# Row statistics of two layer norms, from bn_stats on VectorE to sums on VectorE and squared deviations on ScalarE

## The chip, the cores and the metric

The kernel runs on one core of a Trainium2 chip. The metric is the device time of one execution in microseconds, lower is better. A core has TensorE (PE, with its weight loads shown apart as PEld), VectorE (DVE), ScalarE (ACT), GpSimd (POOL) and SyncE (SP, which here only issues DMAs). Each engine works through its own instructions in order; engines wait for each other through semaphores.

## The reference

Sixteen graphs (batches) of 1024 nodes with 256 features pass through two graph layers, each followed by a residual and a layer norm over the 256 features:

```python
e_k   = leaky(einsum('bid,bjd->bij', h * a_k, h))            # layer 0
alpha = sigmoid(where(adj == 1, e_0, -max)); ...             # adj is 0 or 1 here
x = layernorm(x + einsum('bij,bjd->bid', alpha, h) + bias)
Hh = x @ W                                                   # layer 1
e  = where(adj != 0, exp(-leaky_relu(s[:, None] + d[None, :])), 0)
x = layernorm(x + elu(e @ Hh / rowsum(e)))
def layernorm(x): m = mean(x); v = var(x); return (x - m) / sqrt(v + 1e-5)
```

A row has one mean and one variance in each of the two norms. There are 16 x 1024 rows, that is 16 x 8 tiles of 128 rows, for each norm.

## The kernel before

The order of the work is written out by hand: every engine's instructions stand in the order in which the Python code calls them. The main loop is over batches b = 1 to 15. One turn of the loop does layer 0 of batch b beside layer 1 of batch b - 1 (`prev`) and the end of batch b - 2 (`done`):

1. **Strips** (L757 to L796, jt = 0 to 7). PE computes one strip of scores (L254), upper triangle only; ACT takes two tanh of it (L262 `tb`, L263 `low`); DVE takes the maximum (L264), applies the mask (L270, `finish`) and turns 32 x 32 blocks (L290, `dump`). SP writes the turned strip to DRAM (`mir<-tb`) and one strip later reads it back as the mirrored lower triangle (`al<-mir`, L298, `gather`). Beside it PE projects tiles of `prev` (L558) and ACT evicts them (`project`, `evict_H`: L568 to L570 and L579).
2. **Products** (L816 to L853). Layer 0's sum is a 2 x 2 block product with seven multiplications (L453, banks pQ, pV, pR, pW). DVE masks the gathered blocks (L305, `mask`), combines blocks (L431) and adds up the results (`unite`: L473, L484, L486). The bank pW is used twice: DVE must have read it (L486, `unite(b, "s")`) before PE's product 4 writes it again. Beside it ACT scales tiles of earlier batches (L364) and counts adjacency entries (L130, `check_adj`, a Square with an accumulated sum), and DVE forms layer 1's weights (L619).
3. **Sums** (L856 to L906, t = 0 to 7). PE sums layer 1 of `prev` in eight tiles (L624); the first three are computed together. For each tile DVE inverts the row sum (L660, L661), ACT takes relu and exp (`elu`: L669, L670), and DVE makes the row y = elu + x1 in two instructions (`add`: L675, L677) and then its statistics (`stats`: bn_stats L326, bn_aggr L328). After t = 3 and t = 5 DVE makes the statistics of four tiles of layer 0's rows of batch b (`stats0`, again L326 and L328) and POOL turns them into 1 / sqrt(variance + eps) and the factors that `project` needs (`roots0`: L335 to L359, L401).

`load_adj(b + 1, 1, ...)` at t = 5 issues a load of half of the next adjacency matrix on POOL's queue; a one-element copy (L104) from POOL's own `r_all` makes it wait its turn.

In the last turn (b = 15) there is no next batch: `stats0` and `roots0` come at t = 2 and 3, the projection of batch 15 itself at t = 4 and 6 (its banks come from the pools of the `acc` tiles: tile t = 7 of `acc` gets the bank that the projection's tile 4 had, after ACT's L579 has evicted that), and L600 sends a row of factors through DRAM before the last weights. Then layer 1 of batch 15 runs alone, and `done` = 14 is finished beside it.

Batch 0 is done ahead of the loop (`end0`) and keeps bn_stats in both versions, as do the second norm's rows of batch 15.

Of the kernel before, what the change touches and what calls it, by code (L numbers as in the profile page):

```python
# [10 lines left out]
BF16 = mybir.dt.bfloat16  # L11
U16 = mybir.dt.uint16
I32 = mybir.dt.int32
AF = mybir.ActivationFunctionType
ALU = mybir.AluOpType
AX = mybir.AxisListType
PSUM = bass.MemoryType.PSUM

P = 128
# [4 lines left out]
EPS = 1e-5  # L24
LOW = 1.0e-14
CHECKS = 4
# [4 lines left out]
def one_kind_pass(  # L31
# [296 lines left out]
            nc.vector.bn_aggr(mv, st)  # L328
        return st

    def rstd(mv, what, add_eps=EPS):

        n_t = mv.shape[1]
        ve = small.tile([P, NT], F32, tag="ve", name=f"ve_{what}")[:, 0:n_t]
        nc.gpsimd.tensor_scalar(ve, mv[:, :, 1], add_eps, None, ALU.add)  # L335
        return root_of(ve, what)

    def root_of(ve, what):

# [10 lines left out]

    r_all = {}

    def center(mv, what, add_eps=EPS):

        r = rstd(mv, what, add_eps)
        n = mv.shape[1]
        mr = small.tile([P, NT], F32, tag="mr", name=f"mr_{what}")[:, 0:n]
        nc.gpsimd.tensor_tensor(mr, mv[:, :, 0], r, ALU.mult)
        nc.gpsimd.tensor_scalar(mr, mr, -1.0, None, ALU.mult)  # L359
        r_all[what] = r  # L360
        return [(r[:, t : t + 1], mr[:, t : t + 1]) for t in range(n)]

# [32 lines left out]
    def stats0(b, t):  # L395
        stats(x1s[b][:, t, :], mv0s[b][:, t, :], f"0_{b}_{t}")

    def roots0(b, g):
        r0s[b] += center(mv0s[b][:, ts(g, HT), :], f"0_{b}_{g}", 4.0 * EPS)
        for k, f in enumerate((1.0, -SLOPE, SLOPE - 1.0)):  # L400
            nc.gpsimd.tensor_scalar(  # L401
                rcols[b][:, k, ts(g, HT)], r_all[f"0_{b}_{g}"], f, None, ALU.mult
            )
# [268 lines left out]
    def add(b, t, between=None):  # L672

        y = ys[b][t]
        nc.vector.scalar_tensor_tensor(y, y, 1.0, hs[b, t], ALU.min, ALU.add)  # L675
        if (b, t) != (B - 1, NT - 2):
            nc.vector.scalar_tensor_tensor(y, y, -1.0, x1s[b][:, t, :], ALU.add, ALU.add)  # L677
        if between:
            between()

        full = (b, t) == (B - 1, NT - 2)
        return stats(y, None if full else mv1s[b][:, t, :], f"1_{b}_{t}")

    def scale1(b, t):
        scale(ys[b][t], *r1s[b][t])
# [63 lines left out]
    for b in range(1, B):  # L749
        prev, done = b - 1, b - 2  # L750
        last = b == B - 1

        projects = [[0, 1], [2], [3], [4, 5], [6, 7], [], [], []]
        if prev == 0:

            projects = [[], [], [0, 1], [2, 3], [4, 5, 6, 7], [], [], []]
        for jt in range(NT):  # L757
            if jt == 4:
                mask(b, 0, 0, HT)
                combine_al(b, 1, 0, 2)  # L760
            if jt == 5:
                new_yT(b)
                product(b, 1)
                share_p(prev)
                mask(b, 1, 0, HT)
                combine_al(b, 1, 2, 3)
                mask(b, 0, HT)
                mask(b, 1, HT)
                mask(b, 2, 0, HT)
                combine_al(b, 1, 3, HT)  # L770
                mask(b, 2, HT)
                if done >= 0:
                    r1s[done] = center(mv1s[done], f"1_{done}")
            if jt == 6:
                unite(b, "p1")
                product(b, 5)
                unite(b, "p5")
                mask(b, 3, HT)
                combine_al(b, 2, 0, HT)
            strip(b, jt)  # L780
            finish(b, jt, ends=False)
            if jt < NT - 1:
                dump(b, jt)
            if prev == 0 and jt == 0:
                turn_x1(0, 0)
            if prev == 0 and jt == 1:
                transpose_x1(0)
            if jt >= 1:
                gather(b, jt - 1)
            if jt < 4:  # L790
                combine_x(b, jt)
            for t in projects[jt]:
                project(prev, t)
            if jt == 4:
                evict_H()
            add_twice(b, jt)  # L796
        if not last:
            new_xT(b + 1)
            load_blocks(xTs[b + 1], x[b + 1], 0, N)

        def extras(n):
            if prev == 0 and n < 2:
                scale0(0, HT + 2 * n)
                scale0(0, HT + 2 * n + 1)
            elif prev > 0:
                scale0(prev, 2 * n)
                scale0(prev, 2 * n + 1)
            if done >= 0:
                for q in (2 * n, 2 * n + 1):
                    scale1(done, q)  # L810
                    if q in (3, 7):
                        store(done, q - 3, HT)
            if n < 3:
                check_adj(b, n)

        product(b, 3)  # L816
        combine_al(b, 3, 0, HT)
        extras(0)
        product(b, 6)
        weights(prev, 0)  # L820
        mask(b, 4)
        mask(b, 5)
        combine_al(b, 4, 0, 2)
        weights(prev, 1)
        mask(b, 6)
        combine_al(b, 4, 2, HT)
        unite(b, "u2")
        extras(1)
        product(b, 7)
        extras(2)  # L830
        product(b, 2)
        extras(3)
        unite(b, "s")
        unite(b, "c12")
        unite(b, "c22")
        unite(b, "c11")
        product(b, 4)
        turn_y(b, 0)
        weights(prev, 2)
        weights(prev, 3)  # L840
        weights(prev, 4)
        unite(b, "c21")
        turn_y(b, 1)
        fetch_y(b, 0)
        fetch_y(b, 1)
        if not last:
            load_x(b + 1, [nc.sync])
        check_adj(b, 3)
        weights(prev, 5)
        weights(prev, 6)  # L850
        weights(prev, 7)
        check_pq(prev)
        if not last:  # L853
            load_adj(b + 1, 0, behind=x1s[b][:, HT, 0:1])

        def sum_of(t):  # L856
            homes = {"a": (ps_acc, "acc"), "e": (ps_e, "e"), "t": (ps_t, "t")}
            return acc1(prev, t, *homes[("aaeteeaa" if last else "aaeettat")[t]])

        n_first = 3  # L860
        first = [sum_of(t) for t in range(n_first)]
        for m in range(NT):
            for t in range(n_first):
                sum1(prev, t, first[t], m)
        if not last:
            turn_x(b + 1, 0, False)
            turn_x(b + 1, 1, False)
        rinvs = invert_sums(prev, first)
        for t in range(NT):
            if t >= n_first:  # L870
                acc = sum_of(t)
                for m in range(NT):
                    sum1(prev, t, acc, m)
            if last and t == 7:
                for m in range(4):
                    weights(b, m, 0, HT)
            elu(prev, t, *((first[t], rinvs[t]) if t < n_first else (acc,)))
            if last and t in (2, 3):
                for q in range(HT):
                    stats0(b, (t - 2) * HT + q)  # L880
                roots0(b, t - 2)
            if t >= 1:
                add(prev, t - 1)
            if not last and t in (3, 5):
                for q in range(HT):
                    stats0(b, (t - 3) // 2 * HT + q)
                roots0(b, (t - 3) // 2)
                if t == 5:
                    load_adj(b + 1, 1, behind=r_all[f"0_{b}_1"][:, 0:1])
            if t == 3 and not last:  # L890
                scale_x(b + 1, 0)
                scale_x(b + 1, 1)
            if last and t in (4, 6):
                t0 = (t - 4) // 2 * HT
                for n in range(HT):
                    project(b, t0 + n)
                evict_H()
                share_half(b, t0)
            if last and t in (5, 7):
                for q in range(HT):  # L900
                    scale0(b, (t - 5) // 2 * HT + q)
            if last and t == 7:
                for m in range(4, 6):
                    weights(b, m, 0, HT)
        if not last:
            add(prev, NT - 1)  # L906
# [25 lines left out]
    for m in range(NT):  # L932
        if m in (3, 4):
            weights(last, m + 3, 0, HT)
        if m == 4:
            add(done, NT - 1)
            r1s[done] = center(mv1s[done], f"1_{done}")

        for k in range(3 * m - 15, min(3 * m - 12, NT)) if m >= 5 else []:
            weights(last, k, HT, HT)  # L940
        for t in range(n_first):
            sum1(last, t, first[t], m)
# [484 lines left out]
```

## Time and profile before

| what | value |
|---|---|
| runs | 1222.68, 1223.67, 1224.05 us (median 1223.67) |
| the profiled execution: its time | 1222.76 us |
| its span, first to last instruction | 1221.0 us (clock granted 0.998 of full speed) |
| busy: DVE / ACT / POOL | 1080.9 / 729.9 / 362.8 us |
| bn_stats, L326: y_kept, x (120 and 128 of them) | 428 and 397 ns each |
| bn_aggr, L328 (254) | 182 ns each |
| `add`'s second instruction, L677 (120, y_kept) | 425 ns each |
| `check_adj`, L130, 128 x 2048 (64) | 1991 ns, and a read of the accumulator of 190 ns |
| DMA queues: share of 16 engines' span | 56.1% (SP's issues) and 18.5% (POOL's) |

The span is what the instructions fill; 1.76 us of the execution lie around it. Busy shares are means over the whole run. In a timeline the columns are: start, length (both in us, of a merged row for all its xN instructions), engine, line, operation, out<-in, and in brackets the idle time of the engine before it with what ended it. ACT instructions overlap a little: the next can start before the last ends.

### The profile page before, as it was taken

How to read it: one execution, taken by the hardware profiler on the slowest of the kernel's cores; microseconds unless marked ns; L12 is line 12 of the kernel's file. 1: busy time of each engine (PE TensorE's matmuls, PEld its weight loads, DVE VectorE, ACT ScalarE, POOL GpSimd, SP SyncE). 2: the span in 40 equal slices, each digit the busy share in tenths (PEclk: the TensorE clock that was granted, in tenths of full speed). 3: DMA queues.
4: the chain of work that ended last, by engine and by line, in shares of the span. 5: the costliest groups of instructions: out<-in, count | busy, mean ns of one | idle time of the engine just before them, and what ended most of it. 6: DMA issues, size and time to landing. Idle time of an engine off the chain costs nothing.

```text
span 1221.0 us, 15690 instructions
## 1 busy us (share of the span) xinstructions
PE 1209.4 (99%) x4400; PEld 820.0 (67%) x4400; DVE 1080.9 (89%) x2075; ACT 729.9 (60%) x1686; POOL 362.8 (30%) x730
## 2 busy tenths in 40 slices
PE   9999999999999999999999999999999999999997
PEld 7757657576575766758667485675757657576686
DVE  5699898998989989898998989989899898998867
ACT  4573664656657466574666736666475665746654
POOL 2320333412334122332213333133241233412343
PEclk9999999999999999999999999999999999999999
DMA  9567776798778877787887868878688887787412
GB/s 194 104 132 149 136 151 147 154 180 147 142 159 152 183 140 148 151 158 165 160 165 138 157 142 163 171 135 160 141 165 176 147 148 155 152 186 137 106 52 73
DMA packets 604600, 180.66 MB, mean 148 GB/s; under 512 B 482012, under 2 KB 586968, under 8 KB 604504
## 3 DMA queue, kind: packets, MB, share of 16 engines
q1 hardware_dynamic: 582800, 136.90, 56.1%
q0 software_dynamic: 21008, 42.01, 18.5%
q8 instruction: 37, 0.61, 0.2%
q10 hardware_dynamic: 696, 0.66, 0.2%
q14 instruction: 59, 0.48, 0.1%
HBM read 152.44 MB, written 60.62 MB: 175 GB/s over the span
## 4 chain that ended last, share of the span: by engine, by line
PE 92%; DVE 5%; ACT 1%; DMA 1%; issue 1%; SPq 0%; POOL 0%; ACTq 0%; DVEq 0%; POOLq 0%
PE acc L624 33%; PE pe L254 20%; PE pW L453 9%; PE pV L453 8%; PE pH L558 8%; PE pQ L453 7%; PE pR L453 4%; PE acc L381 2%; DVE e L619 1%; DVE al L431 1%; DVE st L326 1%; DMA al<-mir 0%; DVE yT L486 0%; DVE yT L473 0%; DMA p<-p_row 0%
## 5 line engine op out<-in xcount | busy, mean ns | idle before, releaser
L624 PE MATMUL acc<-H,e 128*128 128x257 f32 x2032 | 444.5, 380 | 0.0
L624 PEld LDWEIGHTS acc<-H,e 128*128 128x128 f32 x2032 | 385.3, 190 | 62.5 <-issue 7.2
L254 PE MATMUL pe<-xa,xT 128*128 128x384 f32 (+1 forms) x720 | 249.5, 486 | 0.0
L254 PEld LDWEIGHTS pe<-xa,xT 128*128 128x128 f32 x720 | 132.8, 190 | 89.7 <-issue 54.3
L284 POOL TENSOR_TENSOR al<-ident,al 128x128 f32<-128x128 f32 x128 | 105.9, 836 | 285.9 <-DVE al L270 285.8
L619 DVE SCALAR_TENSOR_TENSOR e<-p,pq_kept,adj 128x1024 f32<-128x1024 f32 (+1 forms) x136 | 161.1, 1229 | 0.5 <-DMA p<-p_row 0.5
L431 DVE TENSOR_TENSOR al<-al 128x1024 f32<-128x1024 f32 (+2 forms) x105 | 145.5, 1386 | 8.3
L262 ACT ACTIVATE tb<-pe 128x512 f32<-128x512 f32 (+1 forms) x192 | 94.2, 491 | 86.7 <-PE pe L254 80.4
L669 ACT ACTIVATE h<-acc,rinv 128x256 f32<-128x256 f32 x81 | 38.3, 473 | 155.8 <-DVE rinv L661 155.8
L264 DVE TENSOR_TENSOR tb<-tb,low 128x512 f32<-128x512 f32 (+1 forms) x192 | 103.0, 550 | 27.7 <-ACT low L263 27.5
L130 ACT ACTIVATE junk<-adj,minus 128x2048 bf16<-128x2048 bf16 x64 | 127.4, 1991 | 0.0
L558 PE MATMUL pH<-Wx,yT 128*128 128x258 f32 x480 | 116.3, 380 | 0.0
L104 POOL CAST adj<-x 128x1 bf16<-128x1 f32 x15 | 2.8, 188 | 369.2 <-DMA x<-y_rows 262.8
L558 PEld LDWEIGHTS pH<-Wx,yT 128*128 128x128 f32 x480 | 91.2, 190 | 31.1 <-issue 13.4
L453 PE MATMUL pV<-al,S 128*128 128x512 f32 x240 | 108.4, 594 | 1.2 <-ACT tb L262 0.5
L453 PE MATMUL pW<-al,x 128*128 128x512 f32 x240 | 108.8, 596 | 0.4
L453 PE MATMUL pQ<-al,x 128*128 128x512 f32 x240 | 107.9, 592 | 0.0
L270 DVE SCALAR_TENSOR_TENSOR al<-tb,adj 128x512 f32<-128x512 f32 (+7 forms) x132 | 97.8, 741 | 5.0
L263 ACT ACTIVATE low<-pe 128x512 f32<-128x512 f32 (+1 forms) x192 | 93.6, 487 | 1.2 <-DVE tb L264 1.2
L650 ACT ACTIVATE sums<-acc,tiny 128x1 f32<-128x1 f32 x45 | 11.8, 261 | 126.3 <-PE acc L624 126.3
L305 DVE SCALAR_TENSOR_TENSOR al<-al,adj 128x512 f32<-128x512 f32 (+3 forms) x150 | 80.9, 560 | 6.2 <-DMA al<-mir 5.7
L453 PEld LDWEIGHTS pW<-al,x 128*128 128x128 f32 x240 | 44.7, 190 | 60.7 <-issue 49.7
(146 smaller groups left out, 1572.3 us busy)
## 6 DMA issues: line engine op xcount, KB each, us to landing
adj<-in_adjT POOLq DMA_DIRECT2D x30, 1024.0 KB, 8.5
x<-in_x SPq DMA_DIRECT2D x15, 1024.0 KB
y_rows<-Z SPq DMA_DIRECT2D x240, 64.0 KB, 2.0
x<-y_rows SPq DMA_DIRECT2D x30, 512.0 KB, 4.8
out<-y_kept SPq DMA_DIRECT2D x30, 512.0 KB, 3.4
xT<-in_x SPq DMA_DIRECT2D x112, 128.0 KB, 3.9
p<-p_row POOLq DMA_DIRECT2D x15, 512.0 KB, 4.1
mir<-tb SPq DMA_DIRECT2D x60, 112.0 KB, 3.3
```

Of the source, the lines that this page charges most:

```text
L130: nc.scalar.activation(junk, rows, AF.Square, bias=minus1, scale=2.0, accum_out=chk[:, b * CHECKS + n : b * CHECKS + n + 1],)
L254: nc.tensor.matmul(pe[:, 0:w], lhsT=xTs[b][:, c, ts(jt, P)], rhs=xas[b][:, c, ds(jt * P + o, w)], start=(c == 0), stop=(c == ND - 1),)
L262: nc.scalar.activation(tb[:, ds(o, w)], pe[:, 0:w], AF.Tanh, scale=0.5)
L263: nc.scalar.activation(low[:, 0:w], pe[:, 0:w], AF.Tanh, scale=0.5 * SLOPE)
L264: nc.vector.tensor_tensor(tb[:, ds(o, w)], tb[:, ds(o, w)], low[:, 0:w], ALU.max)
L270: nc.vector.scalar_tensor_tensor(als[b][:, jt, c0:c1], tbs[b, jt][:, c0 - jt * P : c1 - jt * P], 1.0, adjs[b, jt // HT][:, jt % HT, c0:c1] ...
L284: nc.gpsimd.tensor_tensor(diag, ident2, diag, ALU.add)
L431: nc.vector.tensor_tensor(out_, in0, in1, ALU.subtract)
L453: nc.tensor.matmul(banks[bank], lhsT=lhs[:, jt, :], rhs=rhs[:, jt, :], start=first and jt == 0, stop=jt == HT - 1, skip_group_check=True,)
L558: nc.tensor.matmul(pt, lhsT=x1Ts[b][:, c, ts(t, P)], rhs=Wx[:, c, :], start=(c == 0), stop=(c == ND - 1),)
L619: nc.vector.scalar_tensor_tensor(e, p_bcs[b][:, cols], q, rows, ALU.mult, ALU.min)
L624: nc.tensor.matmul(acc, lhsT=es[b][:, m, ts(t, P)], rhs=Hs[b][m], start=(m == 0), stop=(m == NT - 1),)
```

## The change

Statistics of the eight tiles of the first norm (batches 1 to 15) and of the second norm (batches 0 to 14) change their form; 240 tiles in all. For the first norm, DVE makes the row sums of four tiles with one reduction (`sums0`). For the second, the second instruction of `add` also gives the row sum as an accumulated output. For both, ACT then computes the sum of squares of (sum - 256 times the row) with one Square with an accumulated sum (`deviation`). The division by 256 is left to `rstd` and `center` on POOL (`unit`). A tile's deviation stands, in ACT's order, later than its sum: at t for the second norm's tile t - 2 (the last two tiles after strips 0 and 1 of the next turn), and two of the first norm's tiles at each of t = 4 to 7. `roots0` moves from t = 3 and 5 to t = 5 and 7. In the last turn four deviations stand at each of t = 2 and 3. The copy ahead of `load_adj(b + 1, 1)` reads a sum of the second half instead of a root, so it no longer stands behind `roots0` on POOL's queue.

All deviations write their unneeded squares to one scratch tile with the tag `tmp`, which `check_adj` uses too. The built order shows that a deviation therefore waits for ACT's own semaphore, that is for the deviation just before it.

The order of PE's and SP's instructions is the same in both versions. DVE has 480 instructions fewer of bn_stats and bn_aggr and 30 reductions more; ACT has 240 deviations more.

```diff
-    def rstd(mv, what, add_eps=EPS):
+    def rstd(mv, what, add_eps=EPS, unit=1.0):
...
-        nc.gpsimd.tensor_scalar(ve, mv[:, :, 1], add_eps, None, ALU.add)
+        if unit == 1.0:
+            nc.gpsimd.tensor_scalar(ve, mv[:, :, 1], add_eps, None, ALU.add)
+        else:
+            nc.gpsimd.tensor_scalar(ve, mv[:, :, 1], unit * unit * unit, add_eps, ALU.mult, ALU.add)
         return root_of(ve, what)
+
+    def deviation(y, sums):
+
+        junk = one.tile([P, NT // CHECKS, N], BF16, tag="tmp", name="dev_junk")
+        nc.scalar.activation(
+            junk[:, 0, 0:D],
+            y,
+            AF.Square,
+            bias=sums[:, 0:1],
+            scale=-1.0 * D,
+            accum_out=sums[:, 1:2],
+        )
...
-    def center(mv, what, add_eps=EPS):
-
-        r = rstd(mv, what, add_eps)
+    def center(mv, what, add_eps=EPS, unit=1.0):
+
+        r = rstd(mv, what, add_eps, unit)
...
-        nc.gpsimd.tensor_scalar(mr, mr, -1.0, None, ALU.mult)
+        nc.gpsimd.tensor_scalar(mr, mr, -unit, None, ALU.mult)
...
+    def sums0(b, g):
+        nc.vector.tensor_reduce(
+            mv0s[b][:, ts(g, HT), 0], x1s[b][:, ts(g, HT), :], AX.X, ALU.add
+        )
+
+    def deviation0(b, t):
+        deviation(x1s[b][:, t, :], mv0s[b][:, t, :])
+
     def roots0(b, g):
-        r0s[b] += center(mv0s[b][:, ts(g, HT), :], f"0_{b}_{g}", 4.0 * EPS)
+        unit = 1.0 / D if b else 1.0
+        r0s[b] += center(mv0s[b][:, ts(g, HT), :], f"0_{b}_{g}", 4.0 * EPS, unit)
...
         nc.vector.scalar_tensor_tensor(y, y, 1.0, hs[b, t], ALU.min, ALU.add)
+        if b < B - 1:
+            nc.vector.scalar_tensor_tensor(
+                y, y, -1.0, x1s[b][:, t, :], ALU.add, ALU.add, accum_out=mv1s[b][:, t, 0:1]
+            )
+            return None
...
+    def deviation1(b, t):
+        deviation(ys[b][t], mv1s[b][:, t, :])
...
-                    r1s[done] = center(mv1s[done], f"1_{done}")
+                    r1s[done] = center(mv1s[done], f"1_{done}", unit=1.0 / D)
...
             if jt < NT - 1:
                 dump(b, jt)
+            if jt < 2 and done >= 0:
+                deviation1(done, NT - 2 + jt)
...
             elu(prev, t, *((first[t], rinvs[t]) if t < n_first else (acc,)))
             if last and t in (2, 3):
+                sums0(b, t - 2)
                 for q in range(HT):
-                    stats0(b, (t - 2) * HT + q)
+                    deviation0(b, (t - 2) * HT + q)
                 roots0(b, t - 2)
             if t >= 1:
                 add(prev, t - 1)
+            if t >= 2:
+                deviation1(prev, t - 2)
             if not last and t in (3, 5):
-                for q in range(HT):
-                    stats0(b, (t - 3) // 2 * HT + q)
-                roots0(b, (t - 3) // 2)
+                sums0(b, (t - 3) // 2)
                 if t == 5:
-                    load_adj(b + 1, 1, behind=r_all[f"0_{b}_1"][:, 0:1])
+                    load_adj(b + 1, 1, behind=mv0s[b][:, HT, 0:1])
+            if not last and t >= 4:
+                for q in range(2 * t - 8, 2 * t - 6):
+                    deviation0(b, q)
+                if t % 2 == 1:
+                    roots0(b, (t - 5) // 2)
...
         if m == 4:
             add(done, NT - 1)
-            r1s[done] = center(mv1s[done], f"1_{done}")
+            for q in (NT - 2, NT - 1):
+                deviation1(done, q)
+            r1s[done] = center(mv1s[done], f"1_{done}", unit=1.0 / D)
```

## The prediction

> **What bounds the kernel now.** I read the page first, then the chain of waits in order of time, then the timelines of ACT, DVE and PE over one turn of the loop. The page:
>
> ```profile
> PE 1209.4 (99%) x4400; PEld 820.0 (67%) x4400; DVE 1080.9 (89%) x2075; ACT 729.9 (60%) x1686; POOL 362.8 (30%) x730
> PE 92%; DVE 5%; ACT 1%; DMA 1%; issue 1%; SPq 0%; POOL 0%; ACTq 0%; DVEq 0%; POOLq 0%
> ```
>
> PE is busy nearly always. Whether it works at its pace is read from repetitions. In the chain of waits:
>
> ```profile
> 551.08 27.81 PE acc L624 x128
> ...
> 625.50 27.81 PE acc L624 x128
> ...
> 700.72 27.81 PE acc L624 x128
> ```
>
> The sums take 27.81 us in each turn, so nothing stalls inside them. From one such line to the next is a turn: 74.42 us here, 75.22 us in the next. The 14 distances (the first line at 102.88, the last at 1149.35 us) are 74.42 to 74.48 six times, else 75.45, 75.00, 75.22, 75.11, 74.78, 74.45, 74.59, 75.28. Above 74.42 that is **4.6 us in all: no more can be won inside the loop**, however much DVE is relieved. [...]
>
> Where those 4.6 us go: to DVE, late before product 4. From the timelines of PE and DVE:
>
> ```profile
> 621.91 3.60 PE L453 MATMUL pW<-al,x 128*128 128x512 f32 x8
> ```
>
> ```profile
> 620.83 0.74 DVE L486 SCALAR_TENSOR_TENSOR yT<-pW,bcol,yT 128x512 f32<-128x512 f32 x1
> 682.15 0.69 DVE L305 SCALAR_TENSOR_TENSOR al<-al,adj 128x512 f32<-128x512 f32 x1 [0.88 <-DMA al<-mir]
> ```
>
> PE may write pW when L486 has read it. It starts at best 70.99 us after the sums' first matmul (550.92); where it starts later, it does so 0.06 us after L486's end. So the deadline for that end is 70.93. L486 ends, in the 14 turns, at 71.85, 71.41, 70.64, 70.72, 70.61, 70.89, 70.65, 71.62, 71.52, 71.19, 70.72, 70.85, 71.00, 71.69. Seven miss it, mostly through a late gather (the second line, 0.88 us in the turn from 625.34); the others have 0.04 to 0.32 us left.
>
> **The relief of DVE.** Per turn go 8 x (428 + 182) and 8 x (397 + 182) ns, 9.5 us; two reductions of 128 x 1024 come, at 1.23 us (L431 reads as many elements), no dearer than four times 420 ns (L189, 256 elements): 2.5 us. The accumulated output of L677 is not in this trace: between nothing and one small instruction (182 ns, L328); I take 0.1 us, 0.8 us a turn. Net some 6 us a turn, all in the sums. (The reduction waits for the same fetched rows as bn_stats, which at 567.54 waited for nothing; it comes about 1 us sooner, and a wait there would come out of the relief.) [...] What comes next for DVE is not earlier:
>
> ```profile
> 579.77 0.47 ACT L670 ACTIVATE y_kept<-acc,rinv 128x256 f32<-128x256 f32 x1
> 580.65 0.60 ACT L262 ACTIVATE tb<-pe 128x512 f32<-128x512 f32 x1 [0.41 <-PE pe L254]
> 581.14 0.59 ACT L263 ACTIVATE low<-pe 128x512 f32<-128x512 f32 x1
> 582.36 0.60 ACT L262 ACTIVATE tb<-pe 128x512 f32<-128x512 f32 x1 [0.63 <-PE pe L254]
> 582.86 0.59 ACT L263 ACTIVATE low<-pe 128x512 f32<-128x512 f32 x1
> ```
>
> ```profile
> 583.48 0.69 DVE L264 TENSOR_TENSOR tb<-tb,low 128x512 f32<-128x512 f32 x1 [0.71 <-ACT low L263]
> ...
> 588.02 0.56 DVE L264 TENSOR_TENSOR tb<-tb,low 128x384 f32<-128x384 f32 x1 [0.21 <-ACT low L263]
> ```
>
> DVE already waits 0.71 us, then 0.21 us, for ACT's `low`. The relief ends in these waits: **gain 0**. After 588.02 DVE has no wait but for gathers until L486, so whatever makes it late there is late at the deadline.
>
> **One deviation on ACT.** The nearest row is a Square with an accumulated sum:
>
> ```profile
> 612.64 1.99 ACT L130 ACTIVATE junk<-adj,minus 128x2048 bf16<-128x2048 bf16 x1
> 614.54 0.19 ACT L130 ACTIVATION_READ_ACCUMULATOR junk<-adj,minus 128x1 f32 x1
> 614.63 1.08 ACT L364 ACTIVATE x<-x,mr,r 128x256 f32<-128x256 f32 x2
> ```
>
> The read starts 0.09 us before the Square's end and the next instruction at that end. L219 (1024 elements, one per-partition operand like L130) takes 1144 ns; from both rows 0.83 ns an element, so 256 take 0.51 us. Bounds: 0.47 (L579) and 0.59 us (L364, two such operands). So 0.51 us if something else follows. If a deviation follows, it waits for the read's end: 0.51 - 0.09 + 0.19 + 0.035 (the gap of L569 behind L568, which it waits for) = 0.645 us.
>
> **In the sums** a tile comes every 3.48 us (16 matmuls of 27.81 / 128 us). ACT has 0.72 us of elu and at most three deviations (1.8 us) in that time, or at t = 3 one deviation and two L219 (2.18 us): all of it fits, in idle time such as the 2.99 us ahead of L669 at 576.27. If a deviation took 0.8 us, three would no longer fit, and t = 7 would begin late as well.
>
> **Strips, 14 turns.** At t = 7 ACT is free at 580.13 (L670's start + 0.36). Three deviations come: 2 x 0.645 + 0.51 = 1.80, so the first L262 starts at 581.93 and no longer waits for PE. The second L263 starts 0.49 + 0.47 + 0.50 later, 583.39 instead of 582.86: 0.53 late. DVE's wait of 0.21 absorbs part; **DVE is 0.32 us late** from strip 1 on. (The deviations after strips 0 and 1 fall into ACT's waits of 0.61, 0.20 and 0.42 us for PE and add under 0.05.) PE itself is not stopped: `pe` has three banks, and the first is read by 583.0, while PE needs it again near 585.6. The gathers' transfers start when DVE has turned a strip, so they shift too. With 0.32 us the seven late turns lose 7 x 0.32 = 2.2 us, the seven others 0.03 + 0.11 + 0 + 0.28 + 0.04 + 0.11 + 0.24 = 0.8 us: **+3.0 us**. Bounds: Squares of 0.59 make the chain 2.04 us and DVE 0.56 late, 3.9 + 2.5 = 6.4 us; no wait between deviations makes it 1.53 us and DVE 0.05 late, 0.4 us.
>
> **The last turn.** There ACT has no idle time from 1170.46 to 1182.6. Reading on from 1162.46, where ACT now waits for `rinv`: DVE's sums0 ends at 1163.43 (the first L677 at 1161.64, + 0.46 + 0.1 + 1.23). Four deviations and one more end at 1163.47 + 4 x 0.645 + 0.51 = 1166.56, elu (0.71) at 1167.27, four and one at 1170.36, elu (0.73) at 1171.09, one at 1171.60. The projection's L568 starts there instead of at 1171.19: 0.41 late; its factors from POOL are there at 1170.1. Two more deviations (t = 5, 6) make it 1.43 late at the eviction whose bank PE's tile t = 7 takes:
>
> ```profile
> 1179.84 0.46 ACT L579 ACTIVATE H<-pH,wr 128x256 f32<-128x256 f32 x1
> ```
>
> ```profile
> 1180.35 5.77 PEld L624 LDWEIGHTS acc<-H,e 128*128 128x128 f32 x27
> ```
>
> It ends at 1180.30 now, 0.05 us before PE's weight load; at 1181.73 it makes PE wait: **+1.4 us** (0.3 without waits between deviations, 2.4 with Squares of 0.59, by the same steps). Behind it L600 (1181.95 + 1.43) lets the weights' first tile end near 1184.3, while PE needs it at 1185.3: covered. PE runs on without a gap to 1212.3, so nothing is given back.
>
> **Moved steps.** `roots0` on POOL takes 4 us; its first half would end near 579 (needed at 583.3), its second near 586 (needed by tile 4's eviction at 594.5): 0, and add_twice (L284) behind it 0.4 us late, which nothing awaits before 598. The adjacency load's copy and issue move from 580.1 to about 574.5 on POOL. Its packets now fill the rings during 582 to 589, when the first `mir` dumps start (586.7); then they would be gone. The late gathers run later still, so I take 0; bounds: all gather waits vanish, or gathers meet the p row's broadcast more often (1 us in a few more turns, +3).
>
> **Sum.** 1222.76 (span 1221.0 + 1.76) + 3.0 + 1.4 = **1227.2 us**. The median of the runs, 1223.67, is 0.9 above the profiled execution; by it 1228.1.
>
> **Rivals.**
> - *Cheap chain:* deviations don't wait for each other. +0.4 and +0.3: 1223.5, no change. For it: ACT overlaps all else; against: the shared scratch tile.
> - *Faster, by the earlier load:* rings free of it let every gather land before DVE comes, and the seven late turns drop to the others' level. Place: L305 behind `al<-mir`. Price: -4.6 from the waits, +0.8 to +1.5 from lateness in all 14 turns, +1.4: 1220.4 to 1221.1. It decides if gathers land by 56 us in a turn (56.8 in the late ones). For it: the load shares the rings with the first dumps. Against: the late gathers are issued at 52 us, 14 us after its last packets.
> - *Dear Squares:* 0.59 us each, as L364; ACT's strip work is in place of DVE's the bound at more turns. 6.4 + 2.4: 1231.6. For it: L364 has the same shape and reads SBUF too; against: it has two per-partition operands, a deviation one.
> - *It doesn't do what it says:* accumulated sums that stall DVE by a Square's time each; absorbed in the sums, 1223 to 1225.
>
> **Chances.** About 0.2%, 2.4 us, is what a measurement of this kernel can tell: slower begins at 1226.1, faster ends at 1221.2. Forecast 0.45, dear Squares 0.13, so slower 0.58. Cheap chain 0.24, doing nothing 0.06: within 0.30. Faster 0.12. Range 1221 to 1232, from the faster rival to the dear Squares.
>
> **What would show it.** Right: Squares near 510 ns, 0.645 us apart; L264's second maximum 0.53 us later against the sums' start, its wait in strip 1 gone; turns of 74.4 to 75.8 us; a PE wait of over 1 us at the last turn's tile 7. Wrong: DVE's wait of 0.21 us still there, turns all at 74.42, or ACT's evictions stopping PE within strips.

## The result, and the profile after

The changed kernel takes 1229.06 us (median of 10 runs, 1226.81 to 1232.89), the kernel before 1223.99 us beside it (10 runs, 1222.68 to 1225.89). The ratio is 1.0041, with a 95% interval of 1.003 to 1.0052: **slower by 0.4%**. Predicted were 1227.2 us and 1221 to 1232. The profiled execution took 1229.39 us, its span is 1227.6.

From the page of the changed kernel, the engines' busy time and the shares of the chain:

```profile
PE 1213.3 (99%) x4400; PEld 820.3 (67%) x4400; DVE 994.8 (81%) x1745; ACT 851.9 (69%) x2166; POOL 380.1 (31%) x730
PE 88%; DVE 5%; ACT 3%; SPq 2%; DMA 2%; issue 1%; POOL 0%; DVEq 0%; ACTq 0%
```

VectorE has 86 us less to do, ScalarE 122 us more, and PE is the bound as before. From the chain of waits, the sums of the turn that the prediction followed, and the start of the next:

```profile
553.76 27.82 PE acc L648 x128
...
628.55 3.47 PE acc L648 x16
```

Again no stall inside the sums, but the turn is 74.79 us where it was 74.42. Over all 14 turns the time above 74.42 us is 9.8 us instead of 4.6. So the span of the profiled execution grew by 6.6 us in three places: **+5.2 us in the loop, +0.7 us behind the last sums' start** (72.43 instead of 71.77 us), and +0.8 us ahead of the first sums. The last is no effect of the change: in the profiles of e1 to e4 and e6 to e8 below, whose work up to there is the same, the first sums start anywhere from 102.3 to 104.9 us. These are single executions, and their waits for gathers differ: with VectorE as punctual as before, e1, e2, e4 and e11 show 4.5 to 5.6 us above 74.42, but e3 shows 4.7 us and e6 8.2 at nearly the same lateness (0.18 and 0.15 us). So one trace tells the loop's loss to about 2 us; by the medians, 5.1 us apart, it is about 4.4.

What happens between the sums and the strips. ScalarE of the changed kernel, whose sums begin at 553.60 us:

```profile
582.44 0.47 ACT L694 ACTIVATE y_kept<-acc,rinv 128x256 f32<-128x256 f32 x1
582.80 0.50 ACT L344 ACTIVATE dev_junk<-y_kept,mv 128x256 bf16<-128x256 f32 x1
583.20 0.20 ACT L344 ACTIVATION_READ_ACCUMULATOR dev_junk<-y_kept,mv 128x1 f32 x1
583.42 0.51 ACT L344 ACTIVATE dev_junk<-x,mv 128x256 bf16<-128x256 f32 x1
...
584.06 0.51 ACT L344 ACTIVATE dev_junk<-x,mv 128x256 bf16<-128x256 f32 x1
...
584.56 0.58 ACT L262 ACTIVATE tb<-pe 128x512 f32<-128x512 f32 x1
585.04 0.59 ACT L263 ACTIVATE low<-pe 128x512 f32<-128x512 f32 x1
```

Three Squares of 0.51 us start 0.62 and 0.64 us apart, because each waits for the accumulator's read before it. The first L262 has lost its wait for PE. VectorE in the same turn (its columns: start, duration, instruction, idle time ahead of it):

```profile
586.63 0.69 DVE L264 TENSOR_TENSOR tb<-tb,low 128x512 f32<-128x512 f32 x1 [0.28 <-ACT low L263]
587.42 1.22 DVE L270 SCALAR_TENSOR_TENSOR al<-tb,adj 128x1024 f32<-128x1024 f32 x1
...
589.71 0.65 DVE L447 TENSOR_TENSOR S<-x 128x512 f32<-128x512 f32 x1
590.29 1.41 DVE L264 TENSOR_TENSOR tb<-tb,low 128x512 f32<-128x512 f32 x2
591.73 1.09 DVE L270 SCALAR_TENSOR_TENSOR al<-tb,adj 128x896 f32<-128x896 f32 x1
592.85 0.98 DVE L290 STREAM_TRANSPOSE tb<-tb 128x768 f32<-128x768 f32 x1
```

Against the sums' start, the second maximum of strip 0 comes at 33.03 us instead of 32.56, and L290 of strip 1 at 39.25 instead of 38.82. L290 in the turn of before, sums from 550.92 us:

```profile
589.74 0.98 DVE L290 STREAM_TRANSPOSE tb<-tb 128x768 f32<-128x768 f32 x1
```

Both waits of before, 0.71 and 0.21 us, have shrunk, to 0.28 us and to nothing; what VectorE saved in the sums stands ahead of strip 0's first maximum, as a new wait of 1.83 us for `low`. L510 (L486 before) ends at 71.04 to 71.31 us even in turns in which no gather is more than 0.1 us late, past its deadline of 70.93.

And GpSimd, where the moved roots still run. The first row is L284 of strip 0 in the turn of before, the others are of the changed kernel:

```profile
585.64 0.45 POOL L284 TENSOR_TENSOR al<-ident,al 128x128 f32<-128x128 f32 x1 [4.18 <-DVE al L270]
...
587.47 1.24 POOL L363 TENSOR_TENSOR r<-r,n 128x4 f32<-128x4 f32 x1
...
589.82 0.86 POOL L284 TENSOR_TENSOR al<-ident,al 128x128 f32<-128x128 f32 x1
```

Here is what the prediction had not seen. L363 works on four columns and takes 0.20 us in the first half's roots; beside VectorE's L270 (587.42 to 588.64) it takes 1.24 and ends 0.07 us after L270. So L284 of strip 0, which waits behind the roots on its queue, starts 36.22 us after the sums' start instead of 34.72 (585.64 us in the turn of before). It begins during VectorE's L447, takes 0.86 us instead of 0.45, and the two maxima of strip 1 take 1.41 us together.

### The profile page after: what moved, and what is told of

It reads as the page before. It is cut to its first block, busy times and chain, and to the rows that moved or that the text cites. A ratio compares the mean times of both kernels' runs of the same rounds, so it can differ in the third digit from the quotient of the medians.

```text
span 1227.6 us, 15871 instructions
## 1 busy us (share of the span) xinstructions
PE 1213.3 (99%) x4400; PEld 820.3 (67%) x4400; DVE 994.8 (81%) x1745; ACT 851.9 (69%) x2166; POOL 380.1 (31%) x730
## 4 chain that ended last, share of the span: by engine, by line
PE 88%; DVE 5%; ACT 3%; SPq 2%; DMA 2%; issue 1%; POOL 0%; DVEq 0%; ACTq 0%
PE acc L648 34%; PE pe L254 18%; PE pW L477 8%; PE pV L477 8%; PE pH L582 7%; PE pQ L477 5%; PE pR L477 4%; PE acc L396 2%; DVE al L455 1%; DMA al<-mir 1%; SPq L294 1%; SPq L525 1%; DVE yT L510 1%; DVE yT L497 1%; DVE al L270 0%
## 5 line engine op out<-in xcount | busy, mean ns | idle before, releaser
L284 POOL TENSOR_TENSOR al<-ident,al 128x128 f32<-128x128 f32 x128 | 111.4, 879 | 207.3 <-DVE al L270 207.2
L264 DVE TENSOR_TENSOR tb<-tb,low 128x512 f32<-128x512 f32 (+1 forms) x192 | 105.8, 570 | 44.6 <-ACT low L263 44.4
L262 ACT ACTIVATE tb<-pe 128x512 f32<-128x512 f32 (+1 forms) x192 | 93.9, 489 | 58.8 <-PE pe L254 56.2
L270 DVE SCALAR_TENSOR_TENSOR al<-tb,adj 128x512 f32<-128x512 f32 (+7 forms) x132 | 97.8, 742 | 5.0
L684 DVE TENSOR_SCALAR rinv<-acc 128x1 f32<-128x1 f32 x82 | 12.8, 156 | 107.0 <-PE acc L648 106.8
L379 ACT ACTIVATE y_kept<-y_kept,mr,r 128x256 f32<-128x256 f32 x120 | 64.9, 588 | 36.3 <-POOL mr L374 35.2
```

The source lines that it names most:

```text
L262: nc.scalar.activation(tb[:, ds(o, w)], pe[:, 0:w], AF.Tanh, scale=0.5)
L264: nc.vector.tensor_tensor(tb[:, ds(o, w)], tb[:, ds(o, w)], low[:, 0:w], ALU.max)
L270: nc.vector.scalar_tensor_tensor(als[b][:, jt, c0:c1], tbs[b, jt][:, c0 - jt * P : c1 - jt * P], 1.0, adjs[b, jt // HT][:, jt % HT, c0:c1] ...
L284: nc.gpsimd.tensor_tensor(diag, ident2, diag, ALU.add)
```

## The experiments

**Theory S:** VectorE's lateness at strip 1 has two parts. Three deviations at t = 7 hold back ScalarE's `low`, and the moved roots push L284 beside VectorE's maxima. VectorE's lateness then misses the deadline for L510. **Rivals:** the earlier adjacency load delays gathers (L); ScalarE's added work costs by its amount (W); ScalarE's chain alone makes the whole delay (A).

All times are medians; "L290" is its start in strip 1 against the sums' start (38.82 us before), the measure of VectorE's lateness, which is the same in all turns to 0.01 us, but for one turn of e7 (38.96).

| kernel | us | before beside it | ratio, 95% interval | L290, late by |
|---|---|---|---|---|
| changed | 1229.06 | 1223.99 | 1.0041, 1.003 to 1.0052 | 39.26, 0.44 |
| e1 first norm only | 1222.48 | 1223.39 | 0.9993, 0.9984 to 1.0002 | 38.82, 0 |
| e2 second norm only | 1222.98 | 1223.39 | 0.9997, 0.9987 to 1.0006 | 38.82, 0 |
| e3 roots sooner | 1224.84 | 1223.39 | 1.0017, 1.0008 to 1.0026 | 39.00, 0.18 |
| e4 nothing at t = 7 | 1223.80 | 1223.39 | 1.0003, 0.9994 to 1.0012 | 38.82, 0 |
| e5 = e3, L284 beside | 1229.56 | 1224.24 | 1.0039, 1.0027 to 1.0052 | 39.12, 0.30 |
| e6 own scratch tiles | 1225.38 | 1224.24 | 1.0008, 0.9998 to 1.0019 | 38.97, 0.15 |
| e7 = e4, L447 in the sums | 1224.49 | 1224.24 | 0.9997, 0.9987 to 1.0007 | 38.82, 0 |
| e8 = before, L423 in the sums | 1226.08 | 1224.24 | 1.0015, 1.0006 to 1.0023 | 38.82, 0 |
| e9 = e7, gathers on GpSimd | 1233.12 | 1223.55 | 1.0083, 1.0069 to 1.0097 | 38.82, 0 |
| e10 = before, gathers on GpSimd | 1234.34 | 1223.55 | 1.0089, 1.0075 to 1.0103 | 38.82, 0 |
| e11 = before + 64 columns | 1222.26 | 1222.72 | 0.9997, 0.9988 to 1.0006 | 38.82, 0 |
| e12 = before + 256 columns | 1224.55 | 1222.72 | 1.0011, 1.0001 to 1.0021 | 39.02, 0.20 |

**e1 and e2: one half of the change each.** In e1 `add` and its statistics are as before; in e2 `stats0` and its place are.

> Only the first norm is changed; the second norm's statistics stay with bn_stats on VectorE. Theory S (three chained deviations at t = 7 hold ScalarE's strip evictions back, and GpSimd's moved roots push L284 onto VectorE's strip-1 maximum): with two deviations at t = 7 ScalarE is free at 30.4 us after the sums' start, before the second pe needs it at 31.4, so VectorE's second strip-1 maximum stays at 37.10 and the turns at the lengths of before: 1224 to 1224.8 us, within 1 us of before. Rival L (the earlier adjacency load delays gathers): the load is as early as in the changed kernel, so +4 to +5 us, 1228 to 1229. Rival W (ScalarE's added work as such): about half of the loss, +2.5 us, 1226.5.

> Only the second norm is changed; the first norm's statistics, its roots and the adjacency load stay as before. Theory S: one deviation of 0.51 us lies at t = 7, in ScalarE's wait of 0.41 us and VectorE's waits; the strip-1 maximum stays at 37.10 to 37.15 us: 1224 to 1224.6 us. Rival L: the load is not earlier, so also 1224. Rival W: half of the loss, +2.5 us, 1226.5.

Neither half costs anything that shows (e1 -0.9 us, -2.0 to +0.2; e2 -0.4, -1.6 to +0.7), the whole costs 5 us: W falls, since halves of the work would cost halves of the time. L falls with e1, which has the earlier load.

**e3 and e4: the same deviations in other places.** Both take the first norm's at t = 4 to 6; e3 keeps three at t = 7, all of the second norm, e4 keeps none there and puts the second norm's last three behind strips 0 to 2. The last turn stays as in the changed kernel (e3's line is shortened here to the loop's case):

```
-            if t >= 2:
-                deviation1(prev, t - 2)
+            for q in {2: (0,), 3: (1,), 4: (2,), 7: (3, 4, 5)}.get(t, ()):   # e3
+                deviation1(prev, q)
...
+                for q in {4: (0, 1, 2), 5: (3, 4), 6: (5, 6, 7)}.get(t, ()):  # e3, e4
+                    deviation0(b, q)
+                if t in (5, 6):
+                    roots0(b, t - 5)
```

> The changed kernel with the same number of deviations at t = 7 (three, all of the second norm), but the first norm's last ones at t = 6, so that GpSimd's second roots0 starts one tile earlier and is over before L284 of strip 0. Theory S splits the 0.45 us: VectorE's second strip-0 maximum stays at 33.03 (ScalarE's chain is the same), the first strip-1 maximum falls from 0.86 to 0.68 us, the second comes at 37.37 instead of 37.55; in the turns that is 7 x 0.27 + 0.5 = 2.4 us above before instead of 5.2, with 0.6 us at the last turn 1227.0. Rival A (ScalarE's chain alone makes the whole delay): 37.55 and 1229. Rival L: 1229.

> The changed kernel with the same deviations in other places: none at t = 7 of the loop, three at t = 6, one each behind strips 0, 1 and 2. Theory S: the strip-0 and strip-1 maxima are back at 32.56 and 37.10 us, the turns at the lengths of before; only the last turn keeps its 0.6 us: 1224.0 to 1225. Rival L: the load is as early as in the changed kernel, 1228 to 1229. Rival W: the same work on ScalarE, 1229.

e4 is at the time of before (+0.4 us, -0.7 to +1.5) with all of the work and the earlier load: the cost is one of place. e3 lies between. GpSimd and VectorE of e3, sums from 551.01 us:

```profile
586.19 0.46 POOL L284 TENSOR_TENSOR al<-ident,al 128x128 f32<-128x128 f32 x1 [2.35 <-PE pe L254]
...
587.69 1.15 DVE L264 TENSOR_TENSOR tb<-tb,low 128x512 f32<-128x512 f32 x2
...
590.01 0.98 DVE L290 STREAM_TRANSPOSE tb<-tb 128x768 f32<-128x768 f32 x1
```

With L284 out of the way (it was over by 586.65; GpSimd then idles until 590.05), the two maxima take 1.15 us instead of 1.41, and L290 starts 39.00 us after the sums' start. ScalarE's delay was the same as in the changed kernel, the second maximum of strip 0 at 33.03. So A falls: **of the 0.44 us, ScalarE's chain makes 0.18 and the collision 0.26.** The time came out 2 us below what was expected (1224.8 for 1227). That the lateness was 0.18 and not 0.27 is part of it, some 1 us by the expectation's own sum; the rest lies within the interval.

**e5: the collision put back into e3.** A copy of one column makes GpSimd wait for L447:

```
+            if jt == 0:
...
+                nc.gpsimd.tensor_copy(after_S, Ss[b][:, 0, 0, 0:1])
             add_twice(b, jt)
```

> The kernel of e3 with one addition: a copy of one column on GpSimd makes L284 of strip 0 start when VectorE has ended the strip's L447, so that it lies beside the two strip-1 maxima again. ScalarE's work and the deviations are as in e3. Theory S (the collision on VectorE and GpSimd is worth half of the loss or more): the second strip-1 maximum or what follows it comes 0.2 to 0.3 us later than in e3 and L284 lasts longer than 0.46 us; about +3 us, 1228. Rival A (the difference between e3 and the changed kernel is something else, such as the order of the deviations): as e3, 1224.8.

```profile
589.38 0.77 POOL L284 TENSOR_TENSOR al<-ident,al 128x128 f32<-128x128 f32 x1
...
589.86 1.23 DVE L270 SCALAR_TENSOR_TENSOR al<-tb,adj 128x896 f32<-128x896 f32 x1
```

L284 now lasts 0.77 us and lies beside the second maximum and L270, which takes 1.23 us instead of 1.09. VectorE is 0.12 us later than in e3, less than expected, and the median is back at 1229.56 us, 5.3 us above before (3.3 to 6.4). The six runs lie from 1225.23, the traced one, to 1230.15, so the size is loose, the direction not: a lateness of 0.30 us accounts for some 3 us of it, and a wait of PE in the last turn, as in the changed kernel, for about 1 (from the last sums' start to the end of the span it is 72.90 us, before 71.77).

**e6: a scratch tile of its own for each deviation** (a tag with four buffers instead of the shared one).

> The changed kernel with four scratch tiles of their own for the deviations instead of one shared tile. Theory S with the wait between deviations: they come 0.40 us apart (as L579 does behind others), the chain at t = 7 is 0.3 to 0.5 us shorter, VectorE's second strip-0 maximum comes at 32.6 to 32.8, GpSimd's L284 of strip 0 ends before the first strip-1 maximum, and the loop loses next to nothing: 1224 to 1225. Rival (the spacing of 0.62 to 0.64 us is that of the accumulator's read itself, not of the shared tile): spacing unchanged, 1228 to 1229.

ScalarE of e6 at t = 7:

```profile
581.30 0.51 ACT L344 ACTIVATE dev_junk<-y_kept,mv 128x256 bf16<-128x256 f32 x1
...
581.79 0.50 ACT L344 ACTIVATE dev_junk<-x,mv 128x256 bf16<-128x256 f32 x1
...
582.28 0.50 ACT L344 ACTIVATE dev_junk<-x,mv 128x256 bf16<-128x256 f32 x1
```

0.49 us apart instead of 0.62 to 0.64: the wait for the accumulator's read is the shared tile's doing, not the read's own. (Expected were 0.40.) The strip-0 maximum is 0.19 us late instead of 0.47. L284 did not get ahead of the maxima, as I had expected; the roots shifted with the rest and it still takes 0.86 us. The three measurements fit one sum: the two strip-1 maxima were 0.89 us apart before and are 0.60 apart back to back, so 0.29 us can be absorbed; 0.47 + 0.26 - 0.29 = 0.44 (changed), 0.47 - 0.29 = 0.18 (e3), 0.19 + 0.26 - 0.29 = 0.16 (e6).

**e11 and e12: the price of lateness alone.** The kernel before, with one idle bn_stats on VectorE between strip 1's second maximum and L270:

```
             strip(b, jt)
+            if jt == 1:
...
+                nc.vector.bn_stats(late, xs[b][:, 0, 0:256])   # e11: 0:64
             finish(b, jt, ends=False)
```

> The kernel before with one more instruction on VectorE in strip 1, behind its second maximum: bn_stats of 64 columns, some 0.2 us, whose output nothing reads. It gives the price of VectorE's lateness alone, with no work on ScalarE and no moved roots. Theory S with the deadline of 70.93 us for L510 (L486 in this kernel): 0.2 us late costs 1.7 us in 14 turns (the sum over the turns of before): 1225.7. Rival (a lateness of this size is lost in the waits for gathers, the loss comes from elsewhere): 1224.

> The same with bn_stats of 256 columns, 0.43 us, which makes VectorE as late as it is in the changed kernel (0.45 us). Theory S: +4.6 to +4.9 us, 1228.6 to 1229, the same as the changed kernel without its last turn's 0.7 us. Rival: 1224 to 1225.

Both times are below what was expected, and the trace says why. From e12, sums from 550.81 us:

```profile
588.39 0.42 DVE L783 BATCH_NORM_STATS2 late<-x 128x6 f32<-128x256 f32 x1
588.73 1.07 DVE L270 SCALAR_TENSOR_TENSOR al<-tb,adj 128x896 f32<-128x896 f32 x1
589.84 0.98 DVE L290 STREAM_TRANSPOSE tb<-tb 128x768 f32<-128x768 f32 x1
```

The instruction depends on nothing, starts before the maximum has ended, and L270 starts 0.34 us behind it; VectorE is 0.20 us late in e12 and not at all in e11. My sizes were wrong, the price holds within its interval: by the deadline of 70.93 and the 14 turns of before, 0.20 us costs 1.7 us, measured +1.8 (0.1 to 2.6); 0 costs 0, measured -0.5 (-1.5 to 0.7). By the same sum 0.18 costs 1.5 and 0.44 costs 4.7. With the last turn's 0.7 us in the two kernels that wait there these are 2.2 and 5.4; e3 measured +1.45 (1.0 to 3.2), the change +5.1 (3.7 to 6.4). The traces put the deadline 0.1 us earlier (see below). By that 0.20 costs 2.0, 0.18 costs 1.8 and 0.44 costs 5.4 us, and these too lie within the intervals.

**e7 to e10: can the relief be turned into time?** e7 moves the four L447 of the next batch out of the strips into the room won in the sums; e8 does that to the kernel before, which has less room.

```
-            if jt < 4:
+            if jt < 4 and b == 1:
                 combine_x(b, jt)
...
+            if t == 6 and not last:
+                combine_x(b + 1, 0)
+                combine_x(b + 1, 1)
...
             add(prev, NT - 1)
+            combine_x(b + 1, 2)
+            combine_x(b + 1, 3)
```

> The kernel of e4 with the four L447 of the next batch (0.65 us each) moved on VectorE from strips 0 to 3 into the sums, where the change has made room. If the relief can be used at all, VectorE reaches the strips' later work up to 2.3 us sooner and L510 ends before its deadline also where a gather is late: the turns fall towards 74.42, at most -4.6 us: 1219 to 1221. Rival (the gathers' landing, not VectorE, sets the late turns; VectorE only waits longer for them): 1223 to 1224.

> The kernel before with the same move of the four L423 into the sums and no other change. VectorE has less room in the sums there (its waits at t = 6 and 7 are about 0.5 to 1.3 us each). If the room that the change makes is needed for the move: strip-0 maxima late by 0.5 us or more and a gain smaller than that of e7, 1222 to 1224. Rival: the waits before were room enough, and it gains as much as e7, 1219 to 1221.

e7 gains nothing. VectorE's wait for gathers, in the table of waits, first before and then e7:

```profile
DVE al L305 <- DMA al<-mir: 5.7, 8, 1.2
```

```profile
DVE al L305 <- DMA al<-mir: 24.7, 28, 2.1
```

Most of the 2.3 us a turn that VectorE saves in the strips (four L447, 0.57 us each from start to start) comes back as waits: 19 us more over the turns here, and more for `low` (36.2 instead of 27.5 us). e8, without the change, waits 26.3 us for gathers, so it is the move that ends in them. The second gather is issued 46.35 us after the sums' start in e7 and 46.36 before; strip 0's dump cannot begin sooner, because its last maximum waits for ScalarE (0.53 us for `low` in e7, at 584.18 us) and ScalarE's L262 for PE (75.2 us in the whole of e7). In e8 the strip-0 maximum is 0.4 us late, which strip 1 absorbs; why it loses 1.8 us all the same was not found.

SyncE issues those gathers behind the dumps (in e7 the dumps from 587.36 to 593.56 us, the first gather at 593.73), so e9 and e10 issue the first three from GpSimd (`queue = nc.gpsimd if t < 3 else nc.sync`, behind `add_twice`).

> The kernel of e7 with the gathers of strips 0 to 2 issued by GpSimd (behind L284) instead of SyncE, so that they no longer stand behind the dumps' issues: in e7 the second gather was issued 46.35 us after the sums' start, 2.9 us after its dump had landed. If SyncE's queue is what sets the gathers, they land 1 to 3 us sooner, VectorE's waits for them in strips 4 and 5 go, and the room won by the change and by the moved L447 becomes time: up to -4.6 us, 1219 to 1221. Rival (the transfers themselves, or GpSimd's own slower issue, set the landing; or PE has no more to win): 1223 to 1225.

> The kernel before with the same three gathers on GpSimd and nothing else changed, the control to e9. If only the gathers matter, it gains as much as e9, 1219 to 1221; if VectorE's relief is needed to use them, its L510 still ends near 70.6 to 71 us and it gains half or less: 1221.5 to 1224.

Both lose some 10 us, in the loop, though VectorE is not late at strip 1. The medians of the 14 turns, against the sums' start: in e9 the first gather is issued 1.1 us sooner than in e7 (41.0 instead of 42.1) but lands only 0.4 sooner (46.2), and the second is issued and lands later (46.6 and 50.9 us instead of 46.3 and 50.2). Only in 4 turns is the second issued sooner, at 44.5 to 45.2 us; in these the third lands at 54.3 to 55.7 us, where the median of e7 is 53.2. In e10 the second is issued 1.6 us sooner than before, but the third lands 1.4 later. Why the landing does not follow the issue, and what makes up the 10 us, stays open. No version here is faster than the kernel before by more than its interval.

## Why the prediction was right, and where its steps were not

- **The bound** held: PE is busy for 99% of the span in both kernels, and relieving VectorE wins nothing, even where the room is moved into the strips (e7).
- **The deadline** held in kind, and is 0.1 us earlier than 70.93. In each of the changed kernel's 14 turns the next sums start 3.59 us after L510's end; so a turn is longer than 74.42 us when L510 ends after 70.83. The step "where it starts later, it does so 0.06 us after L486's end" looked at the first matmul alone. When PE has waited, the eight matmuls of product 4 take 3.70 us and not the 3.60 of the prediction's row. The kernel before shows it too: in the turn from 625.34 us (first row), and two turns in which L486 ends at 70.85 and 70.89, ahead of 70.93, are 74.45 and 74.48 us long. The other rows are of the changed kernel, sums from 553.60 us:

```profile
697.02 3.70 PE L453 MATMUL pW<-al,x 128*128 128x512 f32 x8
...
624.05 0.74 DVE L510 SCALAR_TENSOR_TENSOR yT<-pW,bcol,yT 128x512 f32<-128x512 f32 x1
...
624.85 3.70 PE L477 MATMUL pW<-al,x 128*128 128x512 f32 x8
```

- **The relief** is as predicted: 86 us in the whole kernel, some 6 us a turn, and no gain. The accumulated L701 takes 424 ns, as without the output (425), and a separate read of 82 ns follows; I had taken 0.1 us. So the output did not lengthen the instruction here.
- **One deviation** of 0.51 us, 0.645 apart, is measured as 0.51 and 0.62 to 0.64. That the shared tile sets the spacing is shown by e6. The rival of the cheap chain is tried by e6: +0.7 us by its working, +1.1 (-0.2 to 2.3) measured, though VectorE was 0.15 us late there and not 0.05.
- **Strips, +3.0 us: the term that was mis-sized, +5.2 in the traces, about 4.4 by the medians.** Three steps failed, not all in one direction. The deadline: at 70.83 the same 0.32 us cost 3.7 us. "DVE's wait of 0.21 absorbs part": 0.29 us were absorbed, since two maxima back to back start 0.60 and not 0.68 us apart, and the second maximum of strip 0 came 0.47 and not 0.53 us late, so ScalarE's chain makes 0.18 us (e3) and not 0.32. And in **"Moved steps"**, "add_twice (L284) behind it 0.4 us late, which nothing awaits before 598": its output was indeed not awaited, but VectorE's maximum beside it was slowed by 0.26 us. The roots were costed by what waits for them, not by what runs beside them. The row behind it is the 0.20 us of L363 that became 1.24 beside L270. L363, which started 0.05 us after L270, ended 0.07 us after it, and the two maxima of strip 1 took 1.41 us instead of the 1.15 of e3 with L284, which had started 0.47 us ahead of the first. That L284's place beside VectorE's instructions costs time is shown by e3 and e5; by what mechanism, and which of two such instructions is slowed, is not shown.
- **The last turn, +1.4 us:** the mechanism was right, the end was not. PE waits at tile 7 for the bank, and resumes 32.68 us after its sums' start instead of 31.30: 1.38 us late.

```profile
1187.84 24.58 PE L648 MATMUL acc<-H,e 128*128 128x257 f32 x112 [0.97 <-ACT H L603]
```

  The end comes only 0.7 us later: the step "PE runs on without a gap to 1212.3, so nothing is given back" left out that before, VectorE and not PE ended the chain there: VectorE formed the last weights (L619) and between them made the statistics of batch 14's last two rows, 0.65 us each, which the change takes away. One of them, in the chain of waits before:

```profile
1190.58 0.44 DVE st L326
```

  In e1, e2 and e6 PE does not wait there and from the last sums' start to the end it is shorter than before (70.90, 71.47 and 71.24 us).
- **The adjacency load, 0,** held (e1, e4).
- **The total:** predicted were 4.4 us above before, measured are 5.1 by the medians; 1227.2 is 1.9 us below the median of 1229.06 and in the range. So close a hit is partly luck: ScalarE's chain was too dear, the collision was missing and the deadline came too late, 2.2 us too little for the loop by the traces, and the last turn was 0.7 us too dear. The start of the profiled execution, 0.8 us later, is chance. The mechanism that was forecast, ScalarE's chain, makes 0.18 of VectorE's 0.44 us; the likeliest case was the right one, but its larger part was not foreseen.

## What to carry to other kernels

Work that is moved to another engine is cheap or dear by where it stands in that engine's queue: three Squares a tile cost nothing in the sums, and three at the hand-over to the strips, with the roots behind them, cost the loop 4 to 5 us. A moved step is to be costed by what it runs beside as well as by who waits for it, as here GpSimd's L284 and L363 beside VectorE's maxima and L270 (1.41 us for two maxima instead of 1.15, 1.24 for L363 instead of 0.20). And ahead of relieving an engine, ask which wait its spare time would end in; here it ended in waits for ScalarE and for DMAs.

## What the runs showed of the hardware that was not expected

- In the changed kernel a GpSimd tensor_tensor on 128 x 4 numbers (L363) took 0.20 us in the first half's roots (at 580.65 us) and 1.24 us in the second's, beside VectorE's L270 (1.22 us from 587.42), and ended 0.07 us after it.
- VectorE instructions overlapped in e11 and e12: a bn_stats of 0.42 us put ahead of L270 (e12) started 0.08 us before the maximum ahead of it ended, L270 started 0.34 us behind it, and L290 came 0.20 us late; one of 0.22 us (e11), which started as early, made it not late at all.
- Two Squares with an accumulated sum started 0.49 us apart with outputs of their own (e6), 0.62 to 0.64 with a shared one (the changed kernel).
